# A cross-attention and RWKV block on one core: values spread to the state's rows by DMA instead of matmul

## The chip, the core and the metric

The kernel runs on one core of a Trainium2 chip. The time is the device time of one execution in microseconds; lower is better. Three executions took 1702.62 to 1706.41 us, with a median of 1705.04 us.

A core has a matrix engine (PE, with its weight loads shown as PEld), a vector engine (DVE), a scalar engine (ACT), a general engine (POOL) and a synchronising engine (SP), which here issues all DMAs. Each runs its own instructions in order; semaphores tie them together. DMAs are carried out by 16 DMA engines.

## What is computed

Sixteen sequences of 112 tokens of width 512 pass through two layers. The first is cross-attention with 16 heads over a context of 375 tokens. The second is an RWKV block: its token mixing is a linear recurrence over a state of 16 x 16 numbers in each of 32 heads. The heart of the second layer is:

```
def step(s, rkvw):
    r_t, k_t, v_t, w_t = rkvw
    a = k_t[..., :, None] * v_t[..., None, :]
    out = jnp.einsum('bhi,bhij->bhj', r_t, u * a + s)
    s = a + w_t[..., :, None] * s
    return (s, out)
...
_, out = jax.lax.scan(step, s0, rkvw)
...
x1 = x + og * g @ Wo.T
...
rr = jax.nn.sigmoid(xr2 @ Wfr.T)
kk = jnp.square(jax.nn.relu(xk2 @ Wfk.T))
return x1 + rr * (kk @ Wfv.T)
```

Row `i` of a head's state belongs to a key channel, column `j` to a value channel. At each token the state decays row by row and gains the outer product of key and value.

## The kernel before

The batch is worked in four groups of four sequences (`N` = 4 x 112 = 448 columns). Activations lie transposed: 128 partitions of a chunk of channels, tokens along the free dimension, four chunks (`NC`). All is fp32.

Two generators produce the work. `attention()` goes through all 16 batches of the first layer, `recurrent(g)` through the second layer of one group. The loop at the end of the kernel pulls both: each `yield` of `recurrent` hands over a number, which is multiplied by `FILL[g]` (1.2, 1.2, 0.9, 0), and attention work of that cost is put in between. Only PE's order is fixed by hand in this way (`manual_schedule`, L665). The order on the other engines, and that of the DMAs on SP, is chosen by a scheduler when the kernel is built. For the last group no attention is left.

The recurrence is computed in 16 steps `n` per group. With `c, e = divmod(n, 4)`, chunk `c` gives the key rows: 8 heads x 16 keys are the 128 partitions. Each step serves four value columns `q` of every head, so that 16 steps cover 4 chunks x 16 value columns. A step has these parts:

- `spread(n)` (L510): every value row has to stand on the 16 partitions of its head's keys. Four matmuls (L517), one for each `q`, with selection matrices of zeros and ones held in `consts` (`C_SEL`), bring this into four PSUM buffers `vb` of the pool `ps_s`. That pool has four buffers and serves the attention's scores (`ps`, L230) and transposed probabilities (`pt`, L253) and the mixing's `pxm` as well.
- `scans(n)` (L523): for each pair of `q`, ACT copies the initial state into the first column of each sequence in `kv` (L535), DVE multiplies `vb` by the keys of the token before into `kv` (L540, two instructions of 444 columns), and DVE scans over time with the decay `w_ps` (L546, two instructions). POOL then multiplies the pair of states by the receptance (L550). `kv` is one tile; the states alternate between `sta` and `stb`.
- `summed(n - 1)` (L554): PE sums the previous step's states over the key rows into `acc`.

Beside it stand `keys`, `values`, `receptances` and `decays` of the next chunk (one project of four matmuls, that is eight in the trace, per step, then copies from PSUM on ACT), and `centred`, `scaled` and `gated` of the chunk before.

In the attention, `scores` gives four `ps`, DVE subtracts them from the mask and takes the minimum (L240), ACT takes exponentials (L243), `transposed` (L249) turns the probabilities on PE into `pt` and DVE copies these to SBUF as `prT` (L257), three copies for each four heads.

DMAs: `slab` (L98) loads a weight of 256 KB into one of eight rotating buffers, `load_context` (L88) a context of 750 KB into a single buffer, which must have been transposed before.

Of the kernel before, what the change touches and what calls it, by code (L numbers as in the profile page):

```python
# [18 lines left out]
GB = 4  # L19
# [12 lines left out]
NR = 19  # L32


C_MEAN, C_GMEAN, C_GSUM, C_WIN, C_SEL = 0, 128, 256, 384, 512
NCONST = C_SEL + NQ * P

# [6 lines left out]
def xattn_rwkv_kernel(ctx: ExitStack, tc: tile.TileContext, ins: dict, out: bass.AP):  # L44
    nc = tc.nc

    def pool(name, bufs, **kw):
        return ctx.enter_context(tc.tile_pool(name=name, bufs=bufs, **kw))
# [8 lines left out]
    big = pool("big", 1)  # L57
    chk = pool("chk", 2)
    tmp = pool("tmp", 4)

    ps_mm = pool("ps_mm", 2, space=PSUM)
    ps_s = pool("ps_s", 4, space=PSUM)
# [186 lines left out]
    def transposed(b, m, c, prs):  # L249

        pt = ps_s.tile([P, 512], F32, tag="s", name=f"pt_{b}_{m}_{c}")
        for hh in range(4):
            nc.tensor.transpose(  # L253
                pt[:SC, hh * T : (hh + 1) * T], prs[hh][:, c * SC : (c + 1) * SC], ident[:T, :T]
            )
        prT = hp.tile([SC, 4, T], F32, tag="prT", name=f"prT_{b}_{m}_{c}")
        nc.vector.tensor_copy(prT, pt[:SC, :N])  # L257
        return prT

    def outputs(b, m, prTs, oR):  # L260
# [96 lines left out]
    def wide(tag, name):  # L357
        return big.tile([P, NC, N], F32, tag=tag, name=name)
# [43 lines left out]
    def recurrent(g):  # L402
# [62 lines left out]
        nc.scalar.activation(thd, pd[:DD, :N], AF.Tanh)  # L465
        yield 1

        ks, vals, rs, owns, ews, w_ps, accs = {}, {}, {}, {}, {}, {}, {}

        def keys(c):  # L470
            ks[c] = chk.tile([P, N], F32, tag="k", name=f"k_{g}_{c}")
# [2 lines left out]
        def values(c):  # L474
            vals[c] = chk.tile([P, N], F32, tag="v", name=f"v_{g}_{c}")
            nc.scalar.copy(vals[c], project("wv1", c, xm[2], f"pv1_{g}_{c}"))

        def receptances(c):
            rs[c] = chk.tile([P, N], F32, tag="r", name=f"r_{g}_{c}")
# [28 lines left out]
        vbs = {}  # L508

        def spread(n):  # L510

            c, e = divmod(n, NQ)
            vbs[n] = []
            for q in range(NQ):
                rows = slice(32 * q, 32 * q + 32)
                vb = ps_s.tile([P, 512], F32, tag="s", name=f"vb_{g}_{n}_{q}")
                nc.tensor.matmul(  # L517
                    vb[:, :N], consts[rows, C_SEL + e * P : C_SEL + (e + 1) * P],
                    vals[c][rows, :], start=True, stop=True,
                )  # L520
                vbs[n].append(vb)

        def scans(n):  # L523

            c, e = divmod(n, NQ)
            st = sts[n % 2]  # L530
            vb = vbs.pop(n)
            kv4 = kv.rearrange("p q (b t) -> p q b t", t=T)
            k_prev = ks[c].rearrange("p (b t) -> p b t", t=T)[:, :, 0 : T - 1]
            for q0 in (0, 2):
                nc.scalar.copy(  # L535
                    kv4[:, q0 : q0 + 2, :, 0],
                    s0[:, c, 4 * q0 + e : 4 * q0 + e + 5 : NQ, :],
                )
                for q in (q0, q0 + 1):
                    nc.vector.tensor_tensor(  # L540
                        kv4[:, q, :, 1:T],
                        vb[q][:, :N].rearrange("p (b t) -> p b t", t=T)[:, :, 0 : T - 1],
                        k_prev, ALU.mult,
                    )
                for q in (q0, q0 + 1):
                    nc.vector.tensor_tensor_scan(  # L546
                        st[:, q, :], w_ps[c], kv[:, q, :], 0.0, ALU.mult, ALU.add
                    )
                pair = st[:, q0 : q0 + 2, :]
                nc.gpsimd.tensor_tensor(  # L550
                    pair, pair, rs[c].unsqueeze(1).broadcast_to([P, 2, N]), ALU.mult
                )
# [134 lines left out]
def _constants():  # L687
    import numpy as np

    c = np.zeros((P, NCONST), np.float32)  # L690
    i = np.arange(P)
    by_i, by_j = i // NS, i % HC
    c[:, C_MEAN : C_MEAN + P] = 1.0 / D
    c[:, C_GMEAN : C_GMEAN + P] = (by_j[:, None] == by_j[None, :]) / NS
    c[:, C_GSUM : C_GSUM + P] = by_i[:, None] == by_j[None, :]
    for e in range(NQ):
        c[i, C_WIN + e * 32 + e * HC + by_i] = 1.0
        c[:, C_SEL + e * P : C_SEL + (e + 1) * P] = (by_j[:, None] == by_i[None, :]) & (
            i[:, None] // HC % NQ == e
        )  # L700
    return c


# [69 lines left out]
```

## Time and profile before

| | value |
|---|---|
| median of three runs | 1705.04 us (1702.62 to 1706.41) |
| the profiled execution | 1716.89 us, span 1714.9 us |
| mean granted PE clock | 0.911 |
| instructions | 18460 |
| DMA | 67.66 MB, mean 39 GB/s |
| four scan stages, us from the span's start | 345 to 560, 765 to 1015, 1178 to 1400, 1500 to 1645 |

A page gives the busy time of each engine as a share of the span. A DVE instruction's row names output and input tiles, its shape, its count, the mean ns of one, and the idle time in front of it with what ended that. A wait "A <- B" is time in which A stood idle until B had finished. Matmul counts are doubled, since an fp32 matmul appears as two. The costliest groups that the change touches, from the page:

```profile
L257 DVE COPY prT<-pt 125x448 f32<-125x448 f32 x192 | 113.4, 614 | 163.7 <-PE pt L253 163.3
...
L540 DVE TENSOR_TENSOR kv<-vb,k 128x444 f32<-128x444 f32 x256 | 142.3, 607 | 65.6 <-PE vb L517 65.4
...
L517 PE MATMUL vb<-v,consts 32*128 32x448 f32 x512 | 108.6, 651 | 29.1 <-DVE mn L240 23.0
L546 DVE TENSOR_TENSOR_SCAN stb<-wp,kv 128x448 f32<-128x448 f32 x128 | 131.4, 1069 | 4.4 <-PE acc L560 2.4
...
L535 ACT COPY kv<-s 128x8 f32<-128x8 f32 x128 | 25.1, 203 | 294.2 <-DVE sta L546 154.8
```

### The profile page before, as it was taken

Reading aid. Unit: us, or ns where it says so; the run is one execution under the profiler, and the core shown is the slowest. Engines: PE = TensorE matmul, PEld = TensorE weight load, DVE = VectorE, ACT = ScalarE, POOL = GpSimd, SP = SyncE. Lnnn points to the kernel's source line nnn. Section 1 sums busy time; section 2 is a strip of 40 time slices with the busy share of each in tenths; the row PEclk is TensorE's granted clock in tenths of the full one; section 3 lists DMA queues with packets and bytes.
Section 4 is the critical chain, followed back from the end, with each engine's and each line's share of the span. In section 5 each row is a group of like instructions: output and inputs, shape, how many; then the busy total and the mean of one; then the engine's idle time right before and its main releaser. Section 6 shows DMA issues by size and latency. Waiting matters only on the chain.

```text
span 1714.9 us, 18460 instructions
## 1 busy us (share of the span) xinstructions
PE 1497.4 (87%) x6784; PEld 742.0 (43%) x6784; DVE 969.7 (57%) x1900; ACT 564.9 (33%) x1276; POOL 415.9 (24%) x290
## 2 busy tenths in 40 slices
PE   6899999888888989989888898998889999698858
PEld 3455554444444445444444444444344444233324
DVE  1344445558768252554867726265787752669942
ACT  2445344223342351522334325142233341212331
POOL 0000002313434010221332411121433410335610
PEclk9899999898888989988889999989889999699789
DMA  7200010011010113101001011201000013011011
GB/s 218 67 20 20 20 51 20 19 26 37 14 43 10 42 49 105 35 13 31 31 20 37 16 51 50 95 6 39 19 19 19 16 44 96 12 37 32 18 37 46
DMA packets 37770, 67.66 MB, mean 39 GB/s; under 512 B 5376, under 2 KB 10496, under 8 KB 37424
## 3 DMA queue, kind: packets, MB, share of 16 engines
q1 hardware_dynamic: 37680, 66.49, 13.2%
q8 instruction: 53, 0.87, 0.2%
q14 instruction: 37, 0.30, 0.1%
HBM read 62.81 MB, written 3.67 MB: 39 GB/s over the span
## 4 chain that ended last, share of the span: by engine, by line
PE 35%; DVE 12%; issue 4%; ACT 3%; DMA 1%; POOL 1%; DVEq 0%; ACTq 0%; POOLq 0%
PE pv L179 3%; PE vb L517 3%; DVE sta L546 3%; PE pk L169 2%; PE pfk L121 2%; DVE stb L546 2%; PE pfv L121 2%; PE pfr L121 2%; PE po L121 2%; PE pv L121 2%; DVE kv L540 2%; PE pt L253 2%; PE pr L121 2%; PE acc L560 2%; PE pg L121 1%
## 5 line engine op out<-in xcount | busy, mean ns | idle before, releaser
L169 PE MATMUL pk<-aT,wk 128*128 128x375 f32 x512 | 200.9, 542 | 12.2 <-DVE qT L292 5.9
L257 DVE COPY prT<-pt 125x448 f32<-125x448 f32 x192 | 113.4, 614 | 163.7 <-PE pt L253 163.3
L550 POOL TENSOR_TENSOR sta<-sta,r 128x896 f32<-128x896 f32 x64 | 132.8, 2086 | 268.4 <-DVE sta L546 266.9
L179 PE MATMUL pv<-wv,aT 128*125 128x512 f32 x384 | 179.0, 612 | 4.3 <-ACT thd L465 2.7
L540 DVE TENSOR_TENSOR kv<-vb,k 128x444 f32<-128x444 f32 x256 | 142.3, 607 | 65.6 <-PE vb L517 65.4
L550 POOL TENSOR_TENSOR stb<-stb,r 128x896 f32<-128x896 f32 x64 | 132.1, 2079 | 170.0 <-DVE stb L546 161.9
L243 ACT ACTIVATE pr<-pr,mn 112x375 f32<-112x375 f32 x256 | 152.4, 596 | 62.9 <-DVE mn L240 62.3
L240 DVE CUSTOM_DVE_ANT_0 pr<-ps,mb 112x375 f32<-112x375 f32 x256 | 126.0, 540 | 63.1 <-PE ps L230 63.1
L253 PE MATMUL pt<-ident,pr 112*125 112x112 f32 x768 | 118.6, 293 | 30.5 <-DVE xm L436 15.7
L169 PEld LDWEIGHTS pk<-aT,wk 128*128 128x128 f32 x512 | 106.6, 218 | 84.8 <-issue 26.1
L253 PEld LDWEIGHTS pt<-ident,pr 112*125 112x125 f32 x768 | 108.7, 204 | 79.9 <-DVE kv L540 29.8
L517 PE MATMUL vb<-v,consts 32*128 32x448 f32 x512 | 108.6, 651 | 29.1 <-DVE mn L240 23.0
L546 DVE TENSOR_TENSOR_SCAN stb<-wp,kv 128x448 f32<-128x448 f32 x128 | 131.4, 1069 | 4.4 <-PE acc L560 2.4
L546 DVE TENSOR_TENSOR_SCAN sta<-wp,kv 128x448 f32<-128x448 f32 x128 | 131.9, 1069 | 2.8 <-PE acc L560 1.4
L535 ACT COPY kv<-s 128x8 f32<-128x8 f32 x128 | 25.1, 203 | 294.2 <-DVE sta L546 154.8
L179 PEld LDWEIGHTS pv<-wv,aT 128*125 128x125 f32 x384 | 71.3, 195 | 84.3 <-issue 78.9
L440 POOL TENSOR_TENSOR xm<-xm,xa 128x448 f32<-128x448 f32 x48 | 56.5, 1197 | 189.1 <-DVE xm L436 177.4
L230 PE MATMUL ps<-kT,qT 32*112 32x375 f32 x512 | 88.4, 546 | 9.0 <-DVE prT L257 3.5
L174 ACT COPY kT<-pk 128x375 f32<-128x375 f32 x64 | 30.0, 468 | 160.1 <-PE pk L169 160.0
L134 DVE BATCH_NORM_STATS2 st<-ctx 125x6 f32<-125x512 f32 x48 | 31.2, 675 | 83.6 <-DMA ctx<-in_ctx 83.6
L517 PEld LDWEIGHTS vb<-v,consts 32*128 32x128 f32 x512 | 42.6, 200 | 78.6 <-DVE mn L240 29.5
L222 POOL TENSOR_SCALAR mb<-mrow 112x375 f32<-112x375 uint8 x16 | 8.4, 522 | 252.2 <-DVE mn L240 164.6
(142 smaller groups left out, 2164.6 us busy)
## 6 DMA issues: line engine op xcount, KB each, us to landing
ctx<-in_ctx SPq DMA_DIRECT2D x16, 750.0 KB
wo<-in_wo SPq DMA_DIRECT2D x32, 256.0 KB
wq<-in_wq SPq DMA_DIRECT2D x16, 256.0 KB
wk<-in_wk SPq DMA_DIRECT2D x16, 256.0 KB
wv<-in_wv SPq DMA_DIRECT2D x16, 256.0 KB
wr<-in_wr SPq DMA_DIRECT2D x16, 256.0 KB
wg<-in_wg SPq DMA_DIRECT2D x16, 256.0 KB
wfk<-in_wfk SPq DMA_DIRECT2D x16, 256.0 KB
```

What stands on the lines that cost most here:

```text
L121: nc.tensor.matmul(ps[:, :N], w[:, k, :], rhs[:, k, :], start=(k == 0), stop=(k == NC - 1))
L169: nc.tensor.matmul(pk[:, :S], wk[:, k, m * P : (m + 1) * P], aT[:, k, :], start=(k == 0), stop=(k == NC - 1),)
L179: nc.tensor.matmul(pv[:SC, :], aT[:, k, c * SC : (c + 1) * SC], wv[:, k, :], start=(k == 0), stop=(k == NC - 1),)
L230: nc.tensor.matmul(ps[:T, :S], qT[r : r + HD, m, t0 : t0 + T], kT[r : r + HD, :], start=True, stop=True,)
L240: nc.vector.tensor_tensor_reduce(pr, pss[hh][:T, :S], mb, 1.0, 3.0e38, ALU.add, ALU.min, mn)
L243: nc.scalar.activation(pr, pr, AF.Exp, bias=mn, scale=-1.0, accum_out=dens[b][:, h : h + 1])
L253: nc.tensor.transpose(pt[:SC, hh * T : (hh + 1) * T], prs[hh][:, c * SC : (c + 1) * SC], ident[:T, :T])
L257: nc.vector.tensor_copy(prT, pt[:SC, :N])
L517: nc.tensor.matmul(vb[:, :N], consts[rows, C_SEL + e * P : C_SEL + (e + 1) * P], vals[c][rows, :], start=True, stop=True,)
L540: nc.vector.tensor_tensor(kv4[:, q, :, 1:T], vb[q][:, :N].rearrange("p (b t) -> p b t", t=T)[:, :, 0 : T - 1], k_prev, ALU.mult,)
L546: nc.vector.tensor_tensor_scan(st[:, q, :], w_ps[c], kv[:, q, :], 0.0, ALU.mult, ALU.add)
L550: nc.gpsimd.tensor_tensor(pair, pair, rs[c].unsqueeze(1).broadcast_to([P, 2, N]), ALU.mult)
```

## The change

Three edits go together. Line numbers of new lines are those of the changed kernel.

The values are spread by DMA. `values(c)` also stores its tile to a DRAM buffer `vd` (two of them rotate); `spread(n)` issues four DMAs on SP (L524), each of which reads eight rows of `vd` and writes every row to 16 partitions of `kv`. There are now two tiles for `kv`, `kva` and `kvb`. The selection matrices and the matmuls with them are gone. `values` comes before `keys` in each chunk.

The keys are multiplied in place. `kv` already holds the values, so one DVE instruction (L544) of 888 columns multiplies a pair of `q` by the keys, in SBUF from SBUF. The ACT copy of the initial state is one for all four `q` (L528), issued in `spread` after the DMAs, which also write those columns.

Of the three copies of transposed probabilities, one (`c` = 1) goes to ACT for the first four batches, and two (`c` = 0 and 2) for the others.

```diff
-        nc.vector.tensor_copy(prT, pt[:SC, :N])
+        if (c == 1) == (b < GB):
+            nc.scalar.copy(prT, pt[:SC, :N])
+        else:
+            nc.vector.tensor_copy(prT, pt[:SC, :N])
...
+    dram = pool("dram", 2, space=bass.MemoryType.DRAM)
...
             nc.scalar.copy(vals[c], project("wv1", c, xm[2], f"pv1_{g}_{c}"))
+            vds[c] = dram.tile([P, N], F32, tag="vd", name=f"vd_{g}_{c}")
+            nc.sync.dma_start(vds[c], vals[c])
...
-        kv = wide("xa", f"kv_{g}")
+        kvs = [wide("xa", f"kva_{g}"), wide("kv", f"kvb_{g}")]
...
             c, e = divmod(n, NQ)
-            vbs[n] = []
+            kv = kvs[n % 2]
+            rows = vds[c].rearrange("(q e h) t -> e h q t", q=NQ, e=NQ)[e]
             for q in range(NQ):
-                rows = slice(32 * q, 32 * q + 32)
-                vb = ps_s.tile([P, 512], F32, tag="s", name=f"vb_{g}_{n}_{q}")
-                nc.tensor.matmul(
-                    vb[:, :N], consts[rows, C_SEL + e * P : C_SEL + (e + 1) * P],
-                    vals[c][rows, :], start=True, stop=True,
-                )
-                vbs[n].append(vb)
+                nc.sync.dma_start(
+                    kv[:, q, 1:N],
+                    rows[:, q, 0 : N - 1].unsqueeze(1).broadcast_to([HC, NS, N - 1]),
+                )
+            nc.scalar.copy(
+                kv.rearrange("p q (b t) -> p q b t", t=T)[:, :, :, 0], s0[:, c, e : NS : NQ, :]
+            )
...
             for q0 in (0, 2):
-                nc.scalar.copy(
-                    kv4[:, q0 : q0 + 2, :, 0],
-                    s0[:, c, 4 * q0 + e : 4 * q0 + e + 5 : NQ, :],
-                )
-                for q in (q0, q0 + 1):
-                    nc.vector.tensor_tensor(
-                        kv4[:, q, :, 1:T],
-                        vb[q][:, :N].rearrange("p (b t) -> p b t", t=T)[:, :, 0 : T - 1],
-                        k_prev, ALU.mult,
-                    )
+                pair = kv4[:, q0 : q0 + 2]
+                nc.vector.tensor_tensor(
+                    pair, pair, k_prev.unsqueeze(1).broadcast_to([P, 2, GB, T - 1]), ALU.mult
+                )
...
-        for part in (keys, values, receptances, decays):
+        for part in (values, keys, receptances, decays):
...
-                (keys, values, receptances, decays)[e](c + 1)
+                (values, keys, receptances, decays)[e](c + 1)
```

The scratch memory reserved for DMA descriptors falls from 4096 to 1024 bytes, and `consts` from 1024 to 512 columns, which makes room for `kvb`.

More of the change, by code (lines that the diff above doesn't have):

```diff
@@ L32 @@
 NR = 19
-C_MEAN, C_GMEAN, C_GSUM, C_WIN, C_SEL = 0, 128, 256, 384, 512
-NCONST = C_SEL + NQ * P
+C_MEAN, C_GMEAN, C_GSUM, C_WIN = 0, 128, 256, 384
+NCONST = C_WIN + NQ * 32
 FILL = (1.2, 1.2, 0.9, 0.0)
@@ L466, in recurrent @@
         yield 1
-        ks, vals, rs, owns, ews, w_ps, accs = {}, {}, {}, {}, {}, {}, {}
+        ks, vals, vds, rs, owns, ews, w_ps, accs = {}, {}, {}, {}, {}, {}, {}, {}
         def keys(c):
@@ L504, in decays_up @@
             )
[L506 removed]
+        kvs = [wide("xa", f"kva_{g}"), wide("kv", f"kvb_{g}")]
         sts = [wide("sx", f"sta_{g}"), wide("x1", f"stb_{g}")]
[L508 removed]
         def spread(n):
             c, e = divmod(n, NQ)
[L513 removed]
+            kv = kvs[n % 2]
+            rows = vds[c].rearrange("(q e h) t -> e h q t", q=NQ, e=NQ)[e]
             for q in range(NQ):
[L515 to L521 removed]
+                nc.sync.dma_start(
+                    kv[:, q, 1:N],
+                    rows[:, q, 0 : N - 1].unsqueeze(1).broadcast_to([HC, NS, N - 1]),
+                )
+            nc.scalar.copy(
+                kv.rearrange("p q (b t) -> p q b t", t=T)[:, :, :, 0], s0[:, c, e : NS : NQ, :]
+            )
         def scans(n):
             c, e = divmod(n, NQ)
[L530 to L532 removed]
+            kv, st = kvs[n % 2], sts[n % 2]
+            kv4 = kv.rearrange("p q (b t) -> p q b t", t=T)[:, :, :, 1:T]
             k_prev = ks[c].rearrange("p (b t) -> p b t", t=T)[:, :, 0 : T - 1]
             for q0 in (0, 2):
[L535 to L544 removed]
+                pair = kv4[:, q0 : q0 + 2]
+                nc.vector.tensor_tensor(
+                    pair, pair, k_prev.unsqueeze(1).broadcast_to([P, 2, GB, T - 1]), ALU.mult
+                )
                 for q in (q0, q0 + 1):
@@ L697, in _constants @@
         c[i, C_WIN + e * 32 + e * HC + by_i] = 1.0
-        c[:, C_SEL + e * P : C_SEL + (e + 1) * P] = (by_j[:, None] == by_i[None, :]) & (
-            i[:, None] // HC % NQ == e
-        )
     return c
@@ L758 @@
     from concourse.bass_utils import run_bass_kernel_spmd
-    nc = bacc.Bacc("TRN2", target_bir_lowering=False, num_devices=1, dynamic_dma_scratch_size=4096)
+    nc = bacc.Bacc("TRN2", target_bir_lowering=False, num_devices=1, dynamic_dma_scratch_size=1024)
     arrays, ins = {}, {}
```

## The prediction

> **What bounds the kernel now.** I read the busy shares first, then the span cut at the four stages in which the scans run, then who waits for whom in those stages, then single instructions. The profiled execution took 1716.89 us for a span of 1714.9 us (2.0 us lie around it); the median of the three runs shown is 1705.04 us, 11.9 us less. I sum on the profiled execution and take those 11.9 us off at the end. A measurement of this kernel tells a change from none at about 0.2% (3.4 us).
>
> Busy shares of the page, then busy time per stage (columns: window, length, then PE, PEld, DVE, ACT, POOL busy us with counts, granted clock, DMA share, GB/s):
>
> ```profile
> PE 1497.4 (87%) x6784; PEld 742.0 (43%) x6784; DVE 969.7 (57%) x1900; ACT 564.9 (33%) x1276; POOL 415.9 (24%) x290
> ...
> 345.00:560.00 215.00, 188.84 (x886) 89.84 (x886) 151.19 (x262) 69.08 (x166) 70.94 (x39) 0.89 0.10 26
> ...
> 765.00:1015.00 250.00, 218.73 (x996) 104.65 (x996) 159.23 (x281) 81.38 (x189) 74.33 (x44) 0.90 0.09 27
> ...
> 1178.00:1400.00 222.00, 200.35 (x1004) 96.54 (x1002) 154.57 (x274) 72.60 (x181) 77.25 (x46) 0.91 0.09 25
> ...
> 1500.00:1645.00 145.00, 127.94 (x434) 48.70 (x433) 116.71 (x160) 38.59 (x81) 70.65 (x36) 0.89 0.11 30
> ```
>
> In the first three scan stages (I call them g0, g1, g2 after their group) PE is busy 88, 87 and 90% with DVE at 64 to 70%: attention work of other batches fills PE, and PE bounds. In the last (g3) there is no attention left; DVE is busy 80%, a step of it takes about 7.1 us (16 steps from 1516.4 to 1630), and its four multiplies and four scans follow each other without gaps: DVE bounds.
>
> **The matmuls that go.** The vb rows alone in those four windows (PE, PEld):
>
> ```profile
> 345.00:560.00 215.00, 25.50 (x128) 9.67 (x128) 0.89 0.10 26
> ...
> 765.00:1015.00 250.00, 25.50 (x128) 10.20 (x128) 0.90 0.09 27
> ...
> 1178.00:1400.00 222.00, 25.44 (x128) 9.83 (x128) 0.91 0.09 25
> ...
> 1500.00:1645.00 145.00, 32.13 (x128) 12.90 (x128) 0.89 0.11 30
> ```
>
> That is 76.4 us of PE in the stages that PE bounds. PE also waits at these matmuls and at the scores and transposes that share their four PSUM buffers (`ps_s`), because DVE has not emptied one. In g1:
>
> ```profile
> PE vb L517 <- DVE mn L240: 9.8, 3, 5.4
> PE pt L253 <- DVE kv L540: 7.3, 2, 5.9
> ...
> PE ps L230 <- DVE kv L540: 1.0, 1, 1.0
> ...
> PE vb L517 <- DVE kv L540: 0.3, 1, 0.3
> ```
>
> 18.4 us there; the same four rows give 17.3 in g0 and 5.6 in g2, 41.3 together. So the most that g0 to g2 can give is 76.4 + 41.3 = 117.7 us.
>
> **The multiply in place.** Before, 256 multiplies of 444 with one input in PSUM: about 35.5 us a stage. After, 128 of 888, both inputs in SBUF. The trace has that shape on DVE, and it has the same kind of operation alone and beside POOL (name, count, min/median/max ns):
>
> ```profile
> L373 DVE TENSOR_TENSOR xa<-x x1: 1091/1091/1091, 1421.8 to 1421.8; 128x896 f32<-128x896 f32 x1
> ...
> L388 DVE TENSOR_TENSOR xa<-xa,ln_r x16: 614/617/626, 282.8 to 1470.9; 128x448 f32<-128x448 f32 x16
> ...
> L579 DVE TENSOR_TENSOR o<-o,gr x16: 618/822/2515, 456.7 to 1640.9; 128x448 f32<-128x448 f32 x16
> ```
>
> 32 x 1.09 = 34.9 us a stage: without a neighbour nothing is won or lost. But L579, like L388 an SBUF-by-SBUF multiply of 448, takes up to 2.5 us because it runs in the scan stages. One case, from the timelines of DVE and POOL:
>
> ```profile
> 1570.30 2.20 DVE L579 TENSOR_TENSOR o<-o,gr 128x448 f32<-128x448 f32 x1
> ...
> 1567.91 4.12 POOL L550 TENSOR_TENSOR stb<-stb,r 128x896 f32<-128x896 f32 x2 [3.43 <-DVE stb L546]
> ```
>
> POOL's second multiply ends at 1572.03, and the DVE one ends 0.47 us later: it stood still until POOL was through. The Trainium skill speaks against the change here (SBUF — State Buffer, "SBUF: two separate sides"): a DVE operation with two SBUF inputs and a POOL operation share a port pair, and whichever starts first holds it for its whole instruction. The scans themselves take 1.07 us throughout, their decay being in PSUM. Taken alone, the L388 row makes the edit free; by the rule a multiply that meets POOL costs up to 2.08 us (mean of L550) more. POOL's two multiplies per step start after a pair of scans, just where the next step's two multiplies stand, so meetings are certain; who gets the port is not shown. Ends: 0.3 us a step (DVE always first, only the rest of POOL's running one is waited for) and 4.2 us (both multiplies wait a whole one). I take 2 us, one of the two meeting a POOL multiply; in g3, where DVE's timeline has seven other operations of 0.6 us in four steps, some of them in between, 1.5.
>
> **The DMAs.** Each step now needs four DMAs of 128 x 1788 B (0.92 MB; 256 DMAs and 58.6 MB in all, beside 67.7 MB now) and each chunk one store of 229 KB. No row is like them; the nearest are the context loads, 375 rows of 2 KB:
>
> ```profile
> 1155.50:1162.50 7.00, 3.75 (x19) 1.74 (x17) 2.56 (x5) 0.47 (x1) 2.23 (x2) 1.00 0.30 109
> ```
>
> 109 GB/s at a DMA share of 0.30, that is 5 of 16 engines at 22 GB/s, 94 ns a row. The skill (DMA: Bandwidth & Descriptors, "Why a DMA increments its semaphore by 16 and not by 1") says why: a copy goes over the largest number of engines up to 16 that divides the slowest dimension of both sides, here 125. For a spread the source begins with 8 rows (each given 16 times), so 8 engines: 64 rows each, 64 x 94 x 1788/2048 = 5.3 us a step. Were it spread over 16 as the 128-row weight loads, 2.6 us. A context load took 8.55 us from issue to use for 75 rows per engine, so some 1.5 us come on top. Lower end 2.6 us; upper end, if 16 reads of one DRAM row cost double, 10.5 us. I take 5.3.
>
> A step of g0 to g2 takes 10.5 to 13 us after the change, so this is hidden behind PE; in g3 it stands beside 7 us of DVE and is just hidden: a quarter `q` can be refilled as soon as its own scan of two steps before is done, one step earlier than needed. If that cover goes, each us over about 7 is paid 16 times in g3. SP's issues, 272 at 0.33 us as a weight load, 90 us, fit in 832 us. In SP's queue the spread of step n+2 waits for a scan of step n, and weight loads wait behind it; those are eight slabs deep, several steps ahead. In front of some spreads stand the mask rows and context loads, which wait for POOL and PE (13 waits of 240.6 us in all for the masks), but for work that PE's order has before the scan the spread needs anyway: nothing. Two context loads a stage now share engines with a spread, up to 5.3 us each; DVE waits for contexts already (83.6 us), PE seldom: 6 us in all, from 0 to 30. The store (8 rows an engine at 94 ns, and 1.5) needs about 2.2 us once per chunk, four steps ahead except the first, which is why values come before keys; the first scan of g3 stays where it is (about 1516). The ACT copy of the initial state now waits for all four DMAs with ACT's exponentials and evictions behind it; ACT already waits 282 us for scans at that copy (L535, 64 copies instead of 128 afterwards), so I price it at 0, and at 1 us x 48 where PE gets to see it.
>
> **The copies.** 112 of 192 prT copies go to ACT (16 in the first four batches, 96 later): 69 us less on DVE (0.614 each), 59 us more on ACT (0.53 as L476) at 33%. Neither bounds g0 to g2; cost 0. It offsets part of the port waits there: DVE had 151, 159 and 155 us, less 9 to 12 for copies, plus 32 for 16 x 2 us: 173, 180, 175.
>
> **Sum.** g0 to g2: PE's 76.4 us go. Of the 41.3 us of waits I count none: g0 would be 172 us long at the ceiling, and DVE alone needs 173, so what DVE loses to the port comes back as waits of PE. g3: 16 x 1.5 = +24, less 5.1 (PE's wait on vb there) = +19. Contexts +6. Together -51: 1716.9 - 51 = 1666 for the profiled execution, 1654 as a median.
>
> **Rivals.**
> 1. *The ceiling*: DVE gets the port first nearly always, as it has no semaphore to wait for while POOL does. Then -117.7, plus 16 x 0.3 - 5.1 in g3, some of the waits kept: about -100, 1605. For: POOL starts 0.16 us after the scan ends, DVE at once. Against: POOL's second multiply is ready too and may slip in between.
> 2. *The port decides (slower)*: both multiplies of each step wait a POOL multiply, 4.2 us. DVE then needs 209, 215 and 209 us in g0 to g2, which at 97% full are 215, 222, 215: -35; g3 gets +67 - 5; contexts +6: +33, 1738. It turns slower from about 3.5 us a step, where g3's loss outgrows what g0 to g2 keep. For: L579's maximum. Against: its median of 0.82 us.
> 3. *The transfers decide*: 10.5 us a step and 1.5 of latency make g3 12 us a step, +78; g0 to g2 keep about 40 of their gain: +38, 1743; from about 145 ns a row on it is slower. Against: 94 ns in the row above.
> 4. *Gain eaten evenly*: DVE stands in order behind multiplies whose DMA is not in yet, PE waits for it at scores: within 10 us of no change.
>
> That the matmuls don't go is excluded: the built program has none of them, in an otherwise equal PE order but for keys and values.
>
> **Chances.** Forecast 0.38, ceiling 0.26, port 0.15, transfers 0.14, eaten 0.07. Faster is the first two and half of the last, 0.67; same 0.03; slower 0.30. The forecast's own range is 1625 to 1685; for 8 in 10 it reaches from 1600 to the port's 1740.
>
> **What would show it.** PE loses 512 matmuls and its wait at scores; the L544 multiplies show a minimum near 1.09 us and a median near 2; the g3 stage grows from 145 us to about 165; DMA share in the stages rises from 0.1 to about 0.3. A median near 1.1 us says ceiling; DVE waiting for vd DMAs by tens of us says transfers.

## The result: 0.4% slower

The changed kernel takes 1712.8 us (median of 8 runs, 1710.83 to 1718.51) against 1706.85 us of the kernel before on the same chip (8 runs, 1702.62 to 1709.33): a ratio of 1.0043, 95% interval 1.0027 to 1.006. The forecast was 1654 us.

The profile's page (busy time, then the chain of work that ended last):

```profile
PE 1417.8 (83%) x6272; PEld 701.5 (41%) x6272; DVE 960.9 (56%) x1660; ACT 602.8 (35%) x1324; POOL 442.3 (26%) x290
...
PE 47%; DVE 22%; DMA 17%; ACT 7%; issue 5%; POOL 2%; SPq 1%; DVEq 0%; ACTq 0%; POOLq 0%
PE pv L180 8%; DMA ctx<-in_ctx 6%; PE pk L170 5%; DMA kvb<-vd 5%; DVE stb L548 5%; DVE sta L548 5%; DMA kva<-vd 4%; PE pfk L122 3%; PE pfv L122 3%; PE pfr L122 3%; PE po L122 3%; ACT pr L244 3%; PE pt L254 3%; PE pq L122 3%; PE pp L122 2%
```

512 matmuls are gone. Before, their rows took 108.6 us of PE (76.4 in the first three stages, 32.1 in the last), but PE's busy time fell by 79.6 us only: the matmuls that are left take some 29 us more, at a mean granted clock of 0.902 where it was 0.911. And the span is only 3.3 us shorter than that of the profiled execution before. The spread DMAs (`kva<-vd`, `kvb<-vd`), which were to be hidden, hold 9% of the chain. I cut the span at the same two events in each group as a stage's ends, the activation that writes `thd` and the first matmul with `wo1`. The view by windows of the changed kernel (window, length, then PE, PEld, DVE, ACT, POOL busy with counts, granted clock, DMA share, GB/s):

```profile
344.00:579.00 235.00, 189.70 (x857) 90.61 (x850) 157.57 (x226) 84.04 (x188) 81.84 (x43) 0.90 0.29 94
753.00:985.00 232.00, 189.38 (x857) 91.90 (x857) 155.20 (x227) 84.32 (x187) 82.46 (x43) 0.90 0.29 96
1152.00:1354.00 202.00, 163.20 (x762) 77.42 (x763) 146.25 (x201) 70.83 (x163) 78.78 (x41) 0.88 0.31 99
1481.00:1637.00 156.00, 109.61 (x288) 36.73 (x287) 134.04 (x122) 35.20 (x63) 73.66 (x35) 0.84 0.39 125
```

Before, cut in the same way:

```profile
350.00:592.00 242.00, 212.49 (x960) 101.56 (x961) 154.78 (x272) 80.43 (x185) 73.67 (x43) 0.89 0.10 27
770.00:1014.00 244.00, 213.66 (x960) 102.52 (x961) 155.02 (x272) 80.23 (x184) 73.45 (x43) 0.90 0.10 27
1178.00:1379.00 201.00, 181.23 (x885) 85.66 (x884) 143.57 (x246) 66.83 (x163) 72.11 (x41) 0.90 0.08 22
1504.00:1641.00 137.00, 120.25 (x417) 45.68 (x416) 113.20 (x154) 37.30 (x79) 69.52 (x35) 0.89 0.11 29
```

PE was not busy for 30, 31, 20 and 17 us of these stages; now it idles 45, 43, 39 and 46 us. In g0 to g2 PE's work fell by 65 us and its idle time rose by 47. So these stages gave 18 us where 76 were forecast, and g3 took back 19. (The profiled execution before took 10 us more than the median before. Measured from the kernel with the third edit alone, which is as fast as the one before and whose profiled execution took 1705.21 us, g0 to g2 gave 11 us.) Two groups of waits are new. First ACT and DVE, over the whole span (engine, line, releaser: total us, times, longest):

```profile
ACT kva L528 <- DMA kva<-vd: 130.9, 26, 9.4
...
ACT kvb L528 <- DMA kvb<-vd: 113.9, 26, 6.6
```

and the multiplies' own rows (busy, mean ns, then idle time before them and its releaser), 1.5 us where one alone takes 1.08:

```profile
L544 DVE TENSOR_TENSOR kva<-kva,k 128x888 f32<-128x888 f32 x64 | 94.0, 1475 | 45.7 <-DMA kva<-vd 45.1
...
L544 DVE TENSOR_TENSOR kvb<-kvb,k 128x888 f32<-128x888 f32 x64 | 99.3, 1561 | 23.8 <-DMA kvb<-vd 23.7
```

What the first looks like in g1 (timeline: start, length, instruction, idle time before it and its releaser):

```profile
864.55 4.02 DVE L548 TENSOR_TENSOR_SCAN sta<-wp,kva 128x448 f32<-128x448 f32 x4
...
865.65 3.51 SPq L524 DMA_DIRECT2D kva<-vd  x4
...
870.40 1.43 DVE L544 TENSOR_TENSOR kva<-kva,k 128x888 f32<-128x888 f32 x1 [1.23 <-DMA kva<-vd]
...
873.90 1.08 DVE L544 TENSOR_TENSOR kva<-kva,k 128x888 f32<-128x888 f32 x1 [2.07 <-DMA kva<-vd]
873.90 0.22 ACT L528 COPY kva<-s 128x16 f32<-128x16 f32 x1 [9.12 <-DMA kva<-vd]
874.02 0.54 ACT L591 ACTIVATE g<-pg 128x448 f32<-128x448 f32 x1
...
874.90 0.61 DVE L592 SCALAR_TENSOR_TENSOR g<-g,pg 128x448 f32<-128x448 f32 x1
...
875.43 1.08 DVE L548 TENSOR_TENSOR_SCAN stb<-wp,kvb 128x448 f32<-128x448 f32 x1
...
875.57 1.22 PE L180 MATMUL pv<-wv,aT 128*125 128x512 f32 x1 [3.30 <-DVE g L592]
```

Each of the four scans of `kva` frees a quarter, and the four DMAs of the step after next go out one by one behind them. SP itself takes 0.57 us for one in the median, and waits for a scan between two. The last of them is in 8.25 us after the first was issued. And in DVE's order, which the scheduler chose, the multiplies of step `n + 2` stand right behind the scans of step `n` that free their buffer, and ahead of the scans of step `n + 1` (`stb`, at 875.43). So nearly nothing of DVE's work covers the transfer. In g0 to g2 most steps stand in this order. Both DVE and ACT stand in order in front of it, ACT for 9.12 us at a copy of 0.22 us. Behind the copy stands the gate's evaluation of `pg`, behind that DVE's, and behind that PE, which wants the PSUM buffer. PE's waits for ACT or DVE are many and small (in g1 none over 4.6 us), with over a dozen different releasers; none of those rows names the DMA.

The second, in g3 (DVE, then POOL, same columns):

```profile
1529.91 4.02 DVE L548 TENSOR_TENSOR_SCAN sta<-wp,kva 128x448 f32<-128x448 f32 x4
...
1538.10 4.02 DVE L548 TENSOR_TENSOR_SCAN stb<-wp,kvb 128x448 f32<-128x448 f32 x4
...
1542.56 3.80 DVE L544 TENSOR_TENSOR kva<-kva,k 128x888 f32<-128x888 f32 x2
```

```profile
1540.30 4.12 POOL L552 TENSOR_TENSOR stb<-stb,r 128x896 f32<-128x896 f32 x2 [4.06 <-DVE stb L548]
```

Two multiplies need 2.06 us when POOL is quiet (at 1552.99). Here the first is caught until 1544.4, when POOL's two end, and the pair takes 3.80. But DVE's order is another in most of g3: between the scans that free `kva` and its next multiplies stands the whole step on `kvb`. With the same DMAs, DVE's waits for them at its multiplies are 1.7 us in all of g3, against 19, 21 and 27 us in g0, g1 and g2.

### The profile page after: what moved, and what is told of

Same layout as the page of the kernel before. It is cut to its first block, busy times and chain, and to the rows that moved or that the text cites. A ratio compares the mean times of both kernels' runs of the same rounds, so it can differ in the third digit from the quotient of the medians.

```text
span 1711.6 us, 17731 instructions
## 1 busy us (share of the span) xinstructions
PE 1417.8 (83%) x6272; PEld 701.5 (41%) x6272; DVE 960.9 (56%) x1660; ACT 602.8 (35%) x1324; POOL 442.3 (26%) x290
## 4 chain that ended last, share of the span: by engine, by line
PE 47%; DVE 22%; DMA 17%; ACT 7%; issue 5%; POOL 2%; SPq 1%; DVEq 0%; ACTq 0%; POOLq 0%
PE pv L180 8%; DMA ctx<-in_ctx 6%; PE pk L170 5%; DMA kvb<-vd 5%; DVE stb L548 5%; DVE sta L548 5%; DMA kva<-vd 4%; PE pfk L122 3%; PE pfv L122 3%; PE pfr L122 3%; PE po L122 3%; ACT pr L244 3%; PE pt L254 3%; PE pq L122 3%; PE pp L122 2%
## 5 line engine op out<-in xcount | busy, mean ns | idle before, releaser
L552 POOL TENSOR_TENSOR sta<-sta,r 128x896 f32<-128x896 f32 x64 | 144.5, 2271 | 250.0 <-DVE sta L548 245.9
L180 PE MATMUL pv<-wv,aT 128*125 128x512 f32 x384 | 190.3, 644 | 22.1 <-DVE o L573 6.2
L552 POOL TENSOR_TENSOR stb<-stb,r 128x896 f32<-128x896 f32 x64 | 141.0, 2220 | 156.6 <-DVE stb L548 156.6
L548 DVE TENSOR_TENSOR_SCAN stb<-wp,kvb 128x448 f32<-128x448 f32 x128 | 130.2, 1068 | 9.3 <-PE acc L562 9.3
L548 DVE TENSOR_TENSOR_SCAN sta<-wp,kva 128x448 f32<-128x448 f32 x128 | 130.9, 1070 | 5.3 <-ACT kva L528 5.3
L544 DVE TENSOR_TENSOR kva<-kva,k 128x888 f32<-128x888 f32 x64 | 94.0, 1475 | 45.7 <-DMA kva<-vd 45.1
L544 DVE TENSOR_TENSOR kvb<-kvb,k 128x888 f32<-128x888 f32 x64 | 99.3, 1561 | 23.8 <-DMA kvb<-vd 23.7
L262 DVE COPY prT<-pt 125x448 f32<-125x448 f32 x80 | 49.4, 617 | 86.6 <-PE pt L254 86.4
L260 ACT COPY prT<-pt 125x448 f32<-125x448 f32 x112 | 59.3, 530 | 87.8 <-PE pt L254 87.8
L156 PE MATMUL pa<-ident,ctx 125*128 125x125 f32 x192 | 39.4, 323 | 54.9 <-DVE ctx L141 16.9
L135 DVE BATCH_NORM_STATS2 st<-ctx 125x6 f32<-125x512 f32 x48 | 31.2, 677 | 92.1 <-DMA ctx<-in_ctx 92.1
```

The costliest lines, as they stand in the source:

```text
L180: nc.tensor.matmul(pv[:SC, :], aT[:, k, c * SC : (c + 1) * SC], wv[:, k, :], start=(k == 0), stop=(k == NC - 1),)
L260: nc.scalar.copy(prT, pt[:SC, :N])
L544: nc.vector.tensor_tensor(pair, pair, k_prev.unsqueeze(1).broadcast_to([P, 2, GB, T - 1]), ALU.mult)
L548: nc.vector.tensor_tensor_scan(st[:, q, :], w_ps[c], kv[:, q, :], 0.0, ALU.mult, ALU.add)
L552: nc.gpsimd.tensor_tensor(pair, pair, rs[c].unsqueeze(1).broadcast_to([P, 2, N]), ALU.mult)
```

## The experiments

Theory D: g0 to g2 lose their gain to waits for the spread DMAs, at ACT's copy (there theory A) and at DVE's multiplies. Theory P: they lose it to the port that DVE's multiplies and POOL's multiplies by the receptance share. Rivals are named where they arise. All ratios are to the kernel before on the same chip; one that I give against the changed kernel is the difference of two such ratios, times 1706.85 us. Stages are cut as above, from the profiled execution of each.

| kernel | us | ratio (95%) | g0 | g1 | g2 | g3 |
|---|---|---|---|---|---|---|
| before | 1706.85 | 1 | 242 | 244 | 201 | 137 |
| changed | 1712.8 | 1.0043 (1.0027 to 1.006) | 235 | 232 | 202 | 156 |
| copy on DVE | 1702.78 | 0.9979 (0.9965 to 0.9994) | 228 | 232 | 203 | 157 |
| copy on POOL | 1698.67 | 0.9942 (0.9926 to 0.9958) | 228 | 228 | 204 | 157 |
| before with prT on ACT | 1707.3 | 0.9995 (0.9979 to 1.0012) | 241 | 239 | 200 | 137 |
| changed with prT on DVE | 1706.57 | 0.9996 (0.9971 to 1.0022) | 232 | 232 | 201 | 156 |
| spread twice | 1674.97 | 0.9826 (0.9792 to 0.986) | 218 | 219 | 199 | 157 |
| no POOL multiply | 1656.87 | 0.9726 (0.9687 to 0.9765) | 222 | 225 | 196 | 134 |
| neither | 1583.92 | 0.9302 (0.925 to 0.9354) | 201 | 200 | 177 | 127 |
| before without POOL multiply | 1699.57 | 0.9986 (0.9965 to 1.0007) | 239 | 239 | 204 | 132 |
| keys in PSUM | 1770.22 | 1.0396 (1.0355 to 1.0438) | 227 | 229 | 197 | 140 |
| last group by matmuls | 1669.22 | 0.9797 (0.9762 to 0.9832) | 226 | 228 | 200 | 134 |
| pairs by one DMA | 1765.98 | 1.036 (1.0316 to 1.0404) | 249 | 247 | 219 | 167 |
| four buffers | 1690.62 | 0.9884 (0.9849 to 0.992) | 235 | 241 | 195 | 137 |

### The copy of the initial state off ACT

In `spread` the ACT copy goes, and `scans` begins with it, on DVE in the first kernel and on POOL in the second:

```diff
-            nc.scalar.copy(
-                kv.rearrange("p q (b t) -> p q b t", t=T)[:, :, :, 0], s0[:, c, e : NS : NQ, :]
-            )
...
             kv, st = kvs[n % 2], sts[n % 2]
+            nc.vector.tensor_copy(
+                kv.rearrange("p q (b t) -> p q b t", t=T)[:, :, :, 0], s0[:, c, e : NS : NQ, :]
+            )
```

> The changed kernel with the copy of the initial state (64 of 128x16) moved from ACT to DVE, in front of each step's first multiply. ACT's other instructions keep their order. Theory A (the copy on ACT stands in ACT's order waiting for the four spread DMAs, 192 us in the first three scan stages, and the gates, keys, values and receptances queued behind it come late for PE): those stages get shorter together by 30 to 60 us, the fourth stays near 156 us, total 1655 to 1685. Theory B (the gain is lost on DVE, which waits at its multiplies for the DMAs and for the port): nothing changes but 64 small DVE copies more, total 1705 to 1720.

> The same copy on POOL in place of DVE. Theory A: ACT's queue is free as in the run with DVE, so g0 to g2 gain the same 30 to 60 us; but POOL now waits for the DMAs in front of its multiplies by r, which can make g3 longer by a few us. Total 1660 to 1695. Theory B: no change, 1705 to 1725.

Measured: 11 us less than the changed kernel with the copy on DVE, 17 us less on POOL. The copy on ACT costs that much, so pricing it at 0 was wrong, but 17 is far from the 30 to 60 that theory A asked for. The stages say why: g0 gets 7 us shorter, g1 0 to 4, g2 nothing. Waiting at the copy was only where ACT stood; with the copy on DVE, one timeline of g1 shows the same wait of PE, with DVE as the one that stands in front of the DMA:

```profile
860.83 0.18 DVE L537 COPY kva<-s 128x16 f32<-128x16 f32 x1 [3.37 <-DMA kva<-vd]
860.92 1.08 DVE L544 TENSOR_TENSOR kva<-kva,k 128x888 f32<-128x888 f32 x1
861.91 0.61 DVE L592 SCALAR_TENSOR_TENSOR g<-g,pg 128x448 f32<-128x448 f32 x1
...
862.58 3.63 PE L180 MATMUL pv<-wv,aT 128*125 128x512 f32 x4 [5.84 <-DVE g L592]
```

### The copies of transposed probabilities

The third edit of the change alone, put into the kernel before; and undone in the changed kernel:

```diff
-        nc.vector.tensor_copy(prT, pt[:SC, :N])
+        if (c == 1) == (b < GB):
+            nc.scalar.copy(prT, pt[:SC, :N])
+        else:
+            nc.vector.tensor_copy(prT, pt[:SC, :N])
```

> The kernel before with only the third edit: two of three copies of transposed probabilities on ACT. The prediction priced it at 0. Theory A: within 5 us of before (1702 to 1712), since neither DVE nor ACT bounds g0 to g2. Rival C: the copies on ACT stand behind other work of ACT and hold the PSUM buffers of the scores longer, so that this edit alone costs 10 to 25 us.

> The changed kernel with all copies of transposed probabilities back on DVE. Theory A: with ACT held up at the initial state's copy, the 112 copies behind it on ACT are among the work that comes late, so undoing them gains up to 15 us: 1698 to 1712. Rival C: gains 10 to 25 us. Theory B (DVE is short in the stages): loses 10 us or more, 1722 and up.

Alone it changes nothing (ratio 0.9995), as the prediction had it. In the changed kernel undoing it gains 8 us; the two intervals only just lie apart. The likely reason, not tested on its own, is that ACT, held up at the initial state's copy, has these 112 copies behind it. The same edit can be free in one kernel and cost something in another.

### Transfers and port, one by one and together

The spreads of steps 0 and 1 of a group alone, the rest of its steps multiplying the same buffer again (theory D's cost goes, P's stays):

```diff
-            for q in range(NQ):
+            for q in range(NQ if n < 2 else 0):
                 nc.sync.dma_start(
```

> The changed kernel with the spread DMAs of steps 0 and 1 of each group alone: 14 of 16 steps multiply the same buffer again, so the scanned values are wrong from the third step on; multiplies, scans, copies and POOL's work stay. Theory D (waiting for the spread DMAs, by ACT at the copy of the initial state, 192 us in g0 to g2, and by DVE at the multiplies, 69 us in all, eats the gain of g0 to g2): these stages shorten by 15 to 30 us each, g3 by 0 to 15, total 1630 to 1675. Theory P (the port held by POOL, some 2 us a step on DVE, eats it): little changes, total 1695 to 1712.

No multiply by the receptance on POOL (P's cost goes, D's stays); the same edit in the kernel before is the control:

```diff
-                pair = st[:, q0 : q0 + 2, :]
-                nc.gpsimd.tensor_tensor(
-                    pair, pair, rs[c].unsqueeze(1).broadcast_to([P, 2, N]), ALU.mult
-                )
```

> The changed kernel without the multiply by the receptance (L552 on POOL): the output lacks that factor, and POOL has nothing that can hold the port in a step except the gate's multiply. Theory P: DVE's multiplies fall from a mean of 1.5 us to 1.09, g3 shortens by at least 16 x 1.7 = 27 us (from 156 to below 130), g0 to g2 by 10 to 25 us each, total 1620 to 1670. Theory D: g3 shortens by 20 to 27 us, g0 to g2 by less than 5 each, total 1675 to 1695.

> Control: the kernel before without the multiply by the receptance on POOL (the output lacks that factor). There DVE's multiplies have one input in PSUM. Theory P (what the receptance multiply costs the changed kernel is the port): at most 10 us less than before, 1692 to 1702. If that multiply costs time in itself, as a link between scan and sum, the control gains much of the 45 us that the changed kernel gained without it.

And both edits in the changed kernel:

> The changed kernel with both taken away: the spread DMAs of steps 0 and 1 of a group alone, and no multiply by the receptance on POOL (the output lacks that factor, and the scanned values are wrong from the third step on). If the two causes are all that eats the gain, g0 to g2 fall to 205 to 215, 205 to 215 and 175 to 185 us (before, less the vb matmuls and some of the waits tied to them), g3 to about 125, total 1610 to 1640. If a third thing holds PE back (ACT's and DVE's fixed orders, laid out for another timing), g0 to g2 stay near 218, 219 and 196 and the total is 1645 to 1655.

Measured, against the changed kernel: without most spreads -37 us, without POOL's multiply -54 us, without both -126 us. The control moves by nothing that can be told (0.9965 to 1.0007, so 6 us at most): the multiply by the receptance costs the kernel before next to nothing, and what it costs the changed kernel is its meeting with multiplies from SBUF. It could also cost time as a link between scan and sum, but PE's waits for it in the changed kernel, 27.4 us, all lie in g3, and there the next experiment keeps that link. The two expectations of single causes were each half right: both causes are real. That 37 + 54 is only 91 of the 126 agrees with the rows of the multiplies. Spread twice:

```profile
L544 DVE TENSOR_TENSOR kva<-kva,k 128x888 f32<-128x888 f32 x64 | 117.4, 1860 | 7.1 <-DMA kva<-vd 7.1
L544 DVE TENSOR_TENSOR kvb<-kvb,k 128x888 f32<-128x888 f32 x64 | 112.1, 1776 | 0.0
```

No POOL multiply:

```profile
L544 DVE TENSOR_TENSOR kva<-kva,k 128x888 f32<-128x888 f32 x64 | 68.4, 1076 | 53.5 <-DMA kva<-vd 52.2 <-issue 1.1 <-DVE st L135 0.2
L544 DVE TENSOR_TENSOR kvb<-kvb,k 128x888 f32<-128x888 f32 x64 | 68.2, 1076 | 38.4 <-DMA kvb<-vd 38.2
```

Neither:

```profile
L544 DVE TENSOR_TENSOR kvb<-kvb,k 128x888 f32<-128x888 f32 x64 | 67.7, 1084 | 0.0
L544 DVE TENSOR_TENSOR kva<-kva,k 128x888 f32<-128x888 f32 x64 | 66.8, 1072 | 6.1 <-DMA kva<-vd 6.1
```

128 multiplies at 1.08 us are 138 us. What DVE loses at them is busy time above that, the port, and idle time before them, the DMA. In the changed kernel: 55 + 69 = 124 us. With few spreads: 91 + 7 = 98. Without POOL's multiply: 0 + 90 = 90. Without both: about 6. **Each wait covers part of the other**: a multiply whose data come late finds POOL done more often, and one that never waits for POOL gets to its data earlier and waits for them longer. The whole kernel follows: 26, 34 and 118 us less on DVE at these lines go with 37, 54 and 126 us less in all. PE's idle time in g0 to g2 follows too: it falls by 19, 17 and 63 us. The rest of what these stages gain is in the matmuls themselves, which take less time at a higher granted clock. Without both:

```profile
341.00:542.00 201.00, 180.06 (x856) 87.29 (x850) 140.32 (x226) 85.16 (x187) 9.44 (x11) 0.93 0.14 47
714.00:913.00 199.00, 177.74 (x855) 86.49 (x848) 140.29 (x226) 85.09 (x187) 9.46 (x11) 0.94 0.15 47
1076.00:1253.00 177.00, 155.82 (x763) 75.29 (x763) 131.07 (x201) 70.96 (x163) 6.09 (x9) 0.92 0.13 41
```

Against the changed kernel the same matmuls take 29 us less of PE here; whether the clock rises because PE idles less was not tested. Against the kernel before, g0 to g2 are 110 us shorter and g3 10, near the ceiling that the forecast named (117.7 us in g0 to g2, 122.8 with g3). The sum agrees in part by luck: it was made of 76.4 us of work and 41.3 of idle time, and what fell is 94 and 16. The total also came out below the 1610 to 1640 us expected.

Two readings of the trace are corrected by this. With both gone ACT still waits 136 us at its copy, for scans now, and the full gain is there:

```profile
ACT kva L528 <- DVE sta L548: 71.9, 26, 6.1
ACT kvb L528 <- DVE stb L548: 64.2, 20, 6.3
```

So the size of a wait at a line (245 us for DMAs in the changed kernel) is not its price (11 to 17 us). And no third cause is needed: with nothing to wait for, ACT's and DVE's order does not hold PE back. It sets what a late transfer costs. Whether the order of g3, kept in g0 to g2, would win the 37 us was not tried.

### The keys in PSUM

The port can also be left without leaving work out. ACT copies a chunk's keys to PSUM, and the multiply reads them there:

```diff
-    ps_s = pool("ps_s", 4, space=PSUM)
+    ps_s = pool("ps_s", 3, space=PSUM)
+    ps_k = pool("ps_k", 1, space=PSUM)
...
+            k_ps[c] = ps_k.tile([P, N], F32, tag="kp", name=f"kp_{g}_{c}")
+            nc.scalar.copy(k_ps[c], ks[c])
...
-            k_prev = ks[c].rearrange("p (b t) -> p b t", t=T)[:, :, 0 : T - 1]
+            k_prev = k_ps[c].rearrange("p (b t) -> p b t", t=T)[:, :, 0 : T - 1]
```

> The changed kernel with the keys of a chunk copied to a PSUM bank by ACT (16 copies of 448) where the decays are, and the multiplies reading them there, so that a multiply has one input in SBUF; that bank is taken from the four of the scores and transposes (three are left). Theory P: multiplies fall to a mean near 1.1 us, g3 shortens from 156 to 130 to 137 us; g0 to g2 gain up to 13 us each less what three banks cost PE at the scores; total 1665 to 1695. If the multiplies stay at 1.5 us the port isn't what they wait for, and the total is 1705 or more.

In total a miss, 1770 us, and inside the stages a hit: the multiplies take 1.02 to 1.12 us without exception with POOL's multiply in place, and the stages are 8, 3, 5 and 16 us shorter. That is theory P shown with all the work done. (32 us are less than the 48 that the stages gain without POOL's multiply; but here PE waits 16 to 19 us for DVE at the scores in each of g0 to g2, for want of the bank.) What I had not priced is that the bank is missing outside the stages too. Attention before g0 takes 382.5 us in place of 343.9, with this row, absent there before, first among the causes that the changed kernel lacks:

```profile
PE ps L232 <- DVE mn L242: 20.1, 21, 3.6
```

That idle time is the smaller part: of the 38.6 us, PE's idle time makes 8 and its busy time 31. The score matmuls of four heads, each from 32 partitions, overlap on PE. PE's busy time with scores up to g0, with four banks and with three:

```profile
0.00:344.00 344.00, 27.03 (x192) 0.95 0.18 53
```

```profile
0.00:383.00 383.00, 51.63 (x192) 0.93 0.16 48
```

A single one takes 0.564 us in the median in either kernel: with three banks fewer of them run side by side. The stretches between g0 and g1 and between g1 and g2 grow by 27 and 21 us as well.

### Last group by matmuls

The initial state's copy on POOL, g0 to g2 spread by DMAs, g3 as before the change (the selectors come into the buffer of the contexts, which is free by then):

```diff
+        by_pe = g == NG - 1
+        if by_pe:
+            sel = ctxp.tile([P, NQ * P], F32, tag="ctx", name=f"sel_{g}")
+            nc.sync.dma_start(sel, ins["sel"])
...
+            if by_pe:
+                vbs[n] = []
+                for q in range(NQ):
+                    rows = slice(32 * q, 32 * q + 32)
+                    vb = ps_s.tile([P, 512], F32, tag="s", name=f"vb_{g}_{n}_{q}")
+                    nc.tensor.matmul(
+                        vb[:, :N], sel[rows, e * P : (e + 1) * P],
+                        vals[c][rows, :], start=True, stop=True,
+                    )
...
+                for q in (q0, q0 + 1) if by_pe else ():
+                    nc.vector.tensor_tensor(
+                        kv4[:, q],
+                        vbs[n][q][:, :N].rearrange("p (b t) -> p b t", t=T)[:, :, 0 : T - 1],
+                        k_prev, ALU.mult,
+                    )
```

> The initial state's copy on POOL as in the run with that name, and the last group (g3) spread by matmuls from PSUM as before the change, g0 to g2 by DMAs: g3 back from 156 to about 137 us, the rest as with the copy on POOL. Total about 19 us under that run: 1676 to 1684. If g3's loss were not due to the port but to what went before it, it would stay at 1695 to 1700.

1669.22 us, a ratio of 0.9797 to before: it beats both kernels, the changed one by 2.5% (1.0043 less 0.9797), and is 7 us below the range expected. Its g3 has the matmuls back and takes 134 us:

```profile
1455.00:1589.00 134.00, 119.29 (x418) 46.20 (x418) 112.97 (x154) 32.30 (x47) 72.48 (x49) 0.90 0.11 30
```

DVE's busy time there is 113 us, with the changed kernel's 134 above. In this stage, where PE has time to spare and DVE has none, the matmuls are the cheaper way.

### Pairs by one DMA

Values stored in the order in which a step wants them, and two quarters spread by one DMA, with the initial state's copy on POOL:

```diff
-            nc.sync.dma_start(vds[c], vals[c])
+            nc.sync.dma_start(vds[c].rearrange("(i q) t -> q i t", q=NQ), vals[c])
...
-            rows = vds[c].rearrange("(q e h) t -> e h q t", q=NQ, e=NQ)[e]
-            for q in range(NQ):
+            rows = vds[c].rearrange("(e h q) t -> e h (q t)", q=NQ, e=NQ)[e]
+            flat = kv.rearrange("p q n -> p (q n)")
+            for a in range(0, NQ * N, 2 * N):
                 nc.sync.dma_start(
-                    kv[:, q, 1:N],
-                    rows[:, q, 0 : N - 1].unsqueeze(1).broadcast_to([HC, NS, N - 1]),
+                    flat[:, a + 1 : a + 2 * N],
+                    rows[:, a : a + 2 * N - 1].unsqueeze(1).broadcast_to([HC, NS, 2 * N - 1]),
                 )
```

> The initial state's copy on POOL, and the values stored in another order, so that two quarters are spread by one DMA: two of 447 KB a step in place of four of 224 KB, with half of SP's issues (a step's took 3.5 us of SP). Theory D: the data of a step are in 1.5 to 3 us earlier, DVE's waits at the multiplies fall by a third or more, total 1680 to 1694. Theory P: no change against the run with the copy on POOL, 1695 to 1703.

A clear miss, the wrong way: 71 us more than with four DMAs. SP's timeline in g3, and POOL's, which waits for the last byte:

```profile
1576.17 2.50 SPq L525 DMA_DIRECT2D kva<-vd  x2
```

```profile
1585.74 0.21 POOL L538 COPY kva<-s 128x16 f32<-128x16 f32 x1 [4.00 <-DMA kva<-vd]
```

From first issue to last byte 9.57 us; with four DMAs, in the run with the copy on POOL, it is 7.81:

```profile
1513.93 3.51 SPq L524 DMA_DIRECT2D kva<-vd  x4
```

```profile
1521.74 0.21 POOL L537 COPY kva<-s 128x16 f32<-128x16 f32 x1 [1.34 <-DMA kva<-vd]
```

The first issue also comes one scan later, since a pair's buffer is free only when its second scan is done. Both rows of SP hold its waits for scans: one issue takes 0.57 us in either kernel, so the 3.5 us of SP named above were a misreading, and two issues fewer save 1.1 us. From the start of the last issue, the last byte takes 7.6 us with two DMAs and 4.9 with four. The data are later, not earlier, and the time rises with it: DVE's waits for spreads at its multiplies are 136 us in place of 71. That agrees with theory D, whose sign for this edit I had wrong. Between the moments named the DMA engines were busy 41 to 43%, with four DMAs 45 to 52%; why the larger transfers come later is not settled.

### Four buffers

On top of the kernel with the last group by matmuls: scans in place, the two buffers of scan results used for spread values too, and spreads three steps ahead in g0 to g2:

```diff
-        kvs = [wide("xa", f"kva_{g}"), wide("kv", f"kvb_{g}")]
-        sts = [wide("sx", f"sta_{g}"), wide("x1", f"stb_{g}")]
+        kvs = [wide(tag, f"kv{tag}_{g}") for tag in ("xa", "kv", "sx", "x1")]
...
-            kv, st = kvs[n % 2], sts[n % 2]
+            kv = st = kvs[n % 4]
...
-        spread(0)
+        ahead = 1 if by_pe else 3
+        for n in range(ahead):
+            spread(n)
...
-            if n + 1 < NQ * NC:
+            if by_pe and n + 1 < NQ * NC:
                 spread(n + 1)
             if n:
                 summed(n - 1)
+            if not by_pe and n + ahead < NQ * NC:
+                spread(n + ahead)
```

> The kernel with the last group by matmuls, and its scans written in place, so that the two buffers of scan results serve as buffers of spread values: four in place of two, and spreads issued three steps ahead in g0 to g2 (each waits for the sum of four steps before in place of the scan of two steps before). Theory D: in g0 to g2 the multiplies no longer wait for DMAs, which was worth 33 us in the three stages where 14 of 16 spreads were left out; here 15 to 33 us, total 1638 to 1656. If contention of the transfers themselves, not their lateness, costs the time, it stays at 1665 to 1672; if the spreads waiting in SP's queue hold up the weight loads behind them, it gets slower than 1675.

1690.62 us, some 15 us above the kernel it builds on: in time the third of the outcomes. SP's own waits in its g1 stage (who waits for whom, total, times, longest):

```profile
SPq L541 <- PE acc L586: 45.0, 9, 12.8
SPq L101 <- PE pk L122: 28.5, 3, 13.7
SPq L101 <- PE pg L122: 25.3, 4, 14.4
```

L541 is the spread and L101 the weight loads. Both stand in one queue: a spread waits for a sum with weight loads behind it, and a weight load waits for its slab with spreads behind it. In that stage a multiply of this kernel waits up to 8.2 us for its spread, 2.5 us in the kernel it builds on. But over g0 to g2 the multiplies' waits for spreads fall from 64 to 40 us, and in no row of the trace does PE or its weight loads wait for a weight's DMA. So the queue's order explains the long waits, and not why g0 and g1 are 9 and 13 us longer; that stays open. Whether early spreads on a queue of their own would win the 37 us was not tried; nor was the lateness of the transfers told apart from the bandwidth that they take, as leaving the spreads out removes both.

## Why the prediction was wrong

- **What bounds the kernel**: right. g0 to g2 were PE's; with both new costs gone the kernel falls to 0.93 of before, 119 us, where the ceiling was put at 117.7 to 122.8, though with other terms.
- **The matmuls**: right, 512 fewer. That the others take 29 us more was not foreseen.
- **The multiply in place**: right alone (1.08 us measured, 1.09 taken). At the port the size per step was off in g0 to g2: 2 us taken, 33 us over 48 steps measured, 0.7 us. In g3 it is 22 us over 16 steps, 1.4 us, 1.5 taken. What it costs in g0 to g2 was not put too low: the forecast gave up all 41.3 us of PE's waits for it, and without the port alone these stages are 26 us shorter. (Its reason for giving up all holds for g0 only: by the same sums g1 would be 206 us long at the ceiling and g2 191, with 180 and 175 of DVE.) The median of the multiplies stayed at 1.08 to 1.10, not near 2, since 79 of the 128 stay below 1.2 us.
- **The DMAs**: this is the step that failed, at "so this is hidden behind PE". The rate was right: 175 GB/s at a share of 0.58 around 870 us is 19 GB/s an engine, with 22 taken. What was wrong is the comparison of 5.3 us with a step of 10.5 to 13, and the cover, "one step earlier than needed". A spread can be issued only when the scan of two steps before frees its quarter, the last byte is in 7.8 to 8.3 us after the first issue, and in g0 to g2 DVE's order wants it right behind those scans. In g3, where DVE's order leaves a step between, the cover held. And what waits is not PE, which has other work, but DVE and ACT, which keep an order and have PE's PSUM buffers to empty behind the waiting instruction. 0 was taken. Without most spreads g0 to g2 are 33 us shorter, and without them on top of the port 66 us: of the 110 us that these stages could give, 92 are lost, where the forecast counted on 41. (An issue takes 0.57 us of SP, not 0.33; no run showed a cost of that.)
- **The ACT copy**: "I price it at 0, and at 1 us x 48 where PE gets to see it": 11 to 17 us, a quarter to a third of the upper price.
- **The copies of transposed probabilities**: 0 is right in the kernel before, 8 us in the changed one.
- **g3**: +19 forecast, +19 in the profile, and the cause is the port, as forecast: 156 us with it, 134 without POOL's multiply, 140 with the keys in PSUM, 157 without most spreads.
- **Contexts**: DVE's wait for them rose from 83.6 to 92.1 us, near the +6; not tested alone.
- **The rivals**: nearest is the fourth, "gain eaten evenly", which has the mechanism (DVE in order behind multiplies whose data are not in) and the size (within 10 us of no change). I gave it 0.07. Port and transfers were set up as two rivals of which one decides. In truth neither was large enough for its own rival's price, and each, alone in a kernel, would have left a gain: 0.9826 and 0.9726. They had to be summed as two costs on the same engine, DVE, not weighed against each other.

## What to carry to other kernels

When PE is the bound, ask what empties its PSUM buffers and in what order. A new wait on an in-order engine is paid by whoever needs the instruction behind it, even if the waiting instruction itself is needed late; compare a transfer's time with the time from the moment its buffer is free to the moment its reader stands first in the order, not with the length of a step. A second buffer gives a step of cover only if the reader's order leaves that step between; where a scheduler makes the order, it has to be looked up. And choose an operation's engine by the stage: here the spread by DMA won a little where PE bounds and lost where DVE does.

## What the runs showed of the hardware

- Two waits on one engine hide each other: 37 and 54 us alone, 126 together.
- A DMA that gives each source row to 16 partitions took SP 0.57 us in the median to issue (0.92 at most), where a weight load takes 0.33 to 0.40 in the median.
- Two spreads of 447 KB had their last byte in 7.6 us after the last issue, four of 224 KB in 4.9.
- Where DVE's multiplies from SBUF run beside POOL's, both get longer: DVE's take 1.02 to 3.00 us in the changed kernel, and POOL's 2.25 us in the mean and up to 2.93, where they took 2.08 and at most 2.33 before, and take 2.10 with the keys in PSUM.
- Score matmuls from 32 partitions overlapped on PE: 192 of them took 27 us with four PSUM banks and 52 with three.
- One operand in PSUM frees a DVE multiply of POOL altogether: 1.02 to 1.12 us over 128 of them, with POOL's 128 multiplies running beside.
